# Folding two weight matrices beside the experts: operands of the first step swapped, a turn added, the first two batches' queries as a pair

## The chip, the core and the metric

The kernel runs on one core of one Trainium2 chip. The metric is the device time of one execution in microseconds (us). The core has a TensorE (PE: matmuls and turns; PEld: its weight loads), a VectorE (DVE), a ScalarE (ACT), a GpSimd (POOL) and a SyncE (SP), which here issues most DMAs.

## What is computed

Two layers on x, 8 batches of 100 tokens of 512 numbers, with a context of 361 rows of 128 numbers for each batch. Cut to what matters:

```python
x = x + L0_xattn(layernorm(x), ctx, Wq, Wkv_expand, Wout)   # 16 heads, causal, softmax
x = x + L0_ffn(layernorm(x), Wg, W1, W2, W3)                # 8 experts, each token takes its top 2
x = x + L1_xattn(layernorm(x), ctx, Wq, w_kc_q, w_kc_kv, W_qr, W_kr, Wo)
x = x + L1_ffn(layernorm(x), w_gate_up, w_down)             # rounded to 8-bit steps

# L1_xattn, the part that concerns this case, for each of 16 heads h:
q_hk  = (hidden_q @ Wq.T).reshape(b, s, H, K)               # K = 128
q_big = einsum('bshk,hkq->bshq', q_hk, w_kc_q)              # q: 384
q_r   = einsum('bshq,hqr->bhsr', q_big, W_qr)               # r: 64
```

For one head, q_r is hidden_q times Wq_h.T (512 x 128) times w_kc_q_h (128 x 384) times W_qr_h (384 x 64). None of the three weights depends on the tokens, so the kernel multiplies them first.

## The kernel before

**Tiling.** The 800 tokens stand in seven tiles of 128 rows (the last has 32). TensorE, VectorE and ScalarE run in an order written out by hand in most stages: each engine takes its instructions in the order in which the source issues them, and one that waits holds up what stands behind it on its engine. DMAs and POOL are ordered by the scheduler. `bank()` hands out one of eight PSUM banks in turn. An f32 product appears in the profile as two PE instructions, an f32 turn (a transpose, a product with `ident`) as one.

**Start.** Two products with zeros (L433) run while the first tile of x is loaded. `first_norm` normalizes tiles (statistics on DVE, square root on ACT in L238, scaling on DVE), `take_columns` turns one tile (L253) and copies it to `xnT` (ACT, L254), `keys` makes the first four batches' keys (L224, each copied by ACT in L228). `queries0(b, n)` makes the queries of n batches (L269) and copies them in two halves (ACT, L273): n = 1 moves 100 columns against each piece of `wq_sb`, n = 2 moves 200. Before, batches 0 and 1 have n = 1 each and the others n = 2. Then `first_norm(2, NT)` norms the other five tiles, and the attention of layer 0 goes batch by batch.

**Gate.** The gate's scores are made in two groups, tiles 0 to 4 and tiles 5 and 6. For each group: `gate_columns` turns the tiles (L577, copies L580 on DVE and L582 on ACT), `gate_scores` (L592, L600), `rank_choices` and `give_slots` (a chain of small DVE instructions and two products), and then two scatters for each tile (POOL, L680) put the rows into the experts' slots in DRAM. The last DVE instruction of the chain (L806) tells whether any expert has too many tokens; a branch (L886) follows, which is not taken here. Behind it the experts' rows are fetched (SP, L960).

**The fold.** Two heads are a pair, and there are eight pairs. `fold_load` brings a pair's weights (`wq_p`, `kq_p`, `qr_p`; three buffers of each). For a pair:
- first step: `fold_head` (L705), six products of w_kc_q's pieces (stationary, 128 columns) with W_qr's pieces (64 columns moving); `fold_copy` (L713) copies the result, 128 x 128, to `a_p` on ACT;
- `fold_second` (L723): two products, each into one half of the partitions, stationary `a_p` (64 columns a head), moving `wq_p` (512 columns), copied to `f_p` (ACT, L727);
- `fold_third` (L733): four turns, copied to `wqf` (ACT, L734), which the second attention's queries use.

Pair 0 is folded between the gate's two groups. Pair 1 has its first step before the branch and the rest behind it, beside pair 2. Pairs 3 to 7 are folded one in each of the experts 0 to 4:

```python
gate_and_up(0)
if loaded: part = fold_first(*loaded.pop(0)); ...
quantise_next()
gate_and_up(1)
if part: part = fold_second(*part)
...
gate_and_up(2)
quantise_next(); ... load_expert(e + 2) ...
if part: fold_third(*part)
turned = columns_of(e + 1, slots[e + 1])
```

Here `gate_and_up` makes one of three parts of an expert's hidden values (L1053, 240 columns moving; in part 2, four of its products go into halves of the partitions), `columns_of` turns the next expert's rows (L985, copies L987 on DVE and L989 on ACT), and the down products (L1117) follow. DVE rounds layer 1's weights beside it (`quantise_next`).

Of the kernel before, what the change touches and what calls it, by code (L numbers as in the profile page):

```python
# [12 lines left out]
F32 = mybir.dt.float32  # L13
# [6 lines left out]
P = 128  # L20
# [19 lines left out]
NH1, R1, CQ = 16, 64, 384  # L40
# [10 lines left out]
def tile_kernel(  # L51
# [7 lines left out]
    nc = tc.nc  # L59
# [11 lines left out]
    def bank(dtype=F32):  # L71
        cols = 512 if dtype == F32 else 1024
        return psum.tile([P, cols], dtype, tag="bank", name="bank")
# [11 lines left out]
    ident = keep.tile([P, P], F32, tag="ident", name="ident")  # L85
# [171 lines left out]
    def queries0(b, n, parts=(0, 1)):  # L257
        per = 4 // n
        if parts[0] == 0:
            qT = atw.tile([P, KC, n * S], F32, tag=f"qT{n}", name=f"qT{b}")  # L260
            for i in range(n):
                queries_of[b + i] = qT[:, :, ts(i, S)]
                halves_of[b + i] = qT
        qT = halves_of[b]
        for o0 in [per * i for i in parts if per * i < KC]:
            pq = bank()
            for o in range(o0, o0 + per):
                for c in range(KC):
                    nc.tensor.matmul(  # L269
                        pq[:, ds((o - o0) * n * S, n * S)], wq_sb[:, c, ts(o, P)],  # L270
                        xnT[:, c, ds(b * S, n * S)], start=(c == 0), stop=(c == KC - 1),
                    )
            nc.scalar.activation(  # L273
                qT[:, ds(o0, per), :], pq[:, : KC * S].rearrange("p (c q) -> p c q", c=per),
                AF.Copy, scale=1.0 / math.sqrt(HD0),
            )
# [152 lines left out]
        attn0_values(b, vals.pop(b), pT)  # L429


    for _ in range(2):
        nc.tensor.matmul(bank()[:, :384], zeros[:, :P], zeros[:, :384], start=True, stop=True)  # L433
    first_norm(0, 1)
    take_columns(0)
# [1 line left out]
    first_norm(1, 2)  # L437
    keys(0, 2, KC)
    take_columns(1)
    queries0(0, 1)  # L440
    queries0(1, 1)
    first_norm(2, NT)

    begin(0)
# [254 lines left out]
            nc.sync.dma_start(qr_p[:, j], wqr[2 * i + j].rearrange("(c p) r -> p c r", p=P))  # L699
        return i, wq_p, kq_p, qr_p  # L700

    def fold_head(i, wq_p, kq_p, qr_p, j, pa=None):
        pa = bank() if pa is None else pa
        for c in range(CQ // P):
            nc.tensor.matmul(  # L705
                pa[:, ts(j, R1)], kq_p[:, j, c, :], qr_p[:, j, c, :],
                start=(c == 0), stop=(c == CQ // P - 1),
            )
        return pa

    def fold_copy(i, wq_p, kq_p, qr_p, pa):
        a_p = fw.tile([P, 2 * R1], F32, tag="a_p", name=f"a_p{i}", bufs=2)
        nc.scalar.copy(a_p, pa[:, : 2 * R1])  # L713
        return i, wq_p, a_p

    def fold_first(*loads):
        pa = fold_head(*loads, 0)
        return fold_copy(*loads, fold_head(*loads, 1, pa))

    def fold_second(i, wq_p, a_p):  # L720
        pb = bank()
        for j in range(2):
            nc.tensor.matmul(  # L723
                pb[ds(R1 * j, R1), :], a_p[:, ts(j, R1)], wq_p[:, j, :], start=True, stop=True
            )
        f_p = fw.tile([P, D], F32, tag="f_p", name=f"f_p{i}", bufs=2)
        nc.scalar.copy(f_p, pb)  # L727
        return i, f_p

    def fold_third(i, f_p):  # L730
        pt = bank()
        for c in range(KC):
            nc.tensor.transpose(pt[:, ts(c, P)], f_p[:, ts(c, P)], ident)  # L733
        nc.scalar.copy(wqf[:, :, ts(i, P)], pt.rearrange("p (c r) -> p c r", c=KC))  # L734
# [49 lines left out]
    nc.scalar.activation(sd0[:, 0:1], ln_eps, AF.Exp)  # L784
    for t in range(5, 7):
        gate_norm(t)
    part = fold_second(*part)
    loaded.append(fold_load(pairs_left.pop(0)))
    xT = gate_columns(5, 7)
    fold_third(*part)  # L790
    gate_scores(5, 7, xT)

    loads = loaded.pop(0)
    pa = fold_head(*loads, 0)
    rank_choices(5, 7)
    give_slots(5, 7)

# [64 lines left out]
    def quantise_next():  # L862
        if gate_up_in:
            turn_gate_up(*quantise_gate_up(*gate_up_in.pop(0)))
            if gate_up_left:
                gate_up_in.append(load_gate_up(gate_up_left.pop(0)))
# [98 lines left out]
    def choices(e, got):  # L965
        gates = []
        for i, (xg, _) in enumerate(got):
            n = SLOTS[i][1]
            one = ffw.tile([P, 1], F32, tag="one", name=f"one{e}_{i}", bufs=4)[:n]
            nc.vector.tensor_scalar(one, xg[:, D + 2 : D + 3], float(NE - e), None, ALU.is_equal)  # L970
            gate = ffw.tile([P, 1], F32, tag="gate", name=f"gate{e}_{i}", bufs=4)[:n]
            nc.vector.scalar_tensor_tensor(
                gate, xg[:, D : D + 1], one, xg[:, D + 1 : D + 2], ALU.mult, ALU.add
            )
            place = small.tile([P, 1], I32, tag="place", name=f"place{e}_{i}")[:n]
            nc.vector.tensor_copy(place, xg[:, D + 3 :])
            gates.append((gate, place))
        return gates
# [55 lines left out]
    )  # L1034
    in_order.__enter__()

    part = fold_copy(*loads, fold_head(*loads, 1, pa))
    following = fold_first(*loaded.pop(0))
    part = fold_second(*part)
    following = fold_second(*following)  # L1040
    fold_third(*part)
    fold_third(*following)
    turned = columns_of(0, slots[0])
# [2 lines left out]
    for e in range(NE):  # L1046
# [10 lines left out]
        def gate_and_up(m):  # L1057
            m0, mr = HCH[m]
            pw = bank()
            s = ffw.tile([P, CAP], F32, tag="silu", name="silu")  # L1060
            if m < 2:
                products(pw[:, :CAP], ds(m0, P))
                products(pw[:, ds(CAP, CAP)], ds(UP[m], P))
                nc.scalar.activation(s, pw[:, :CAP], AF.Silu)  # L1064
                nc.vector.tensor_tensor(hT[:, m, :], s, pw[:, ds(CAP, CAP)], ALU.mult)  # L1065
                return
            products(pw[:, :CAP], ds(m0, P))
            for half in range(2):
                products(
                    pw[ds(64 * half, 64), ds(CAP, CAP)], ds(UP64, 64), 2 * half, 2 * half + 2  # L1070
                )
            nc.scalar.activation(s[:mr], pw[:mr, :CAP], AF.Silu)
            nc.vector.tensor_tensor(hT[64:mr, m, :], s[64:mr], pw[mr:, :CAP], ALU.mult)
            up = ffw.tile([64, CAP], F32, tag="up", name="up", bufs=1)
            nc.vector.tensor_copy(up, pw[:64, ds(CAP, CAP)])
            nc.vector.tensor_tensor(up, up, pw[64:, ds(CAP, CAP)], ALU.add)
            nc.vector.tensor_tensor(hT[:64, m, :], s[:64], up, ALU.mult)  # L1077
# [4 lines left out]
        part = None  # L1082
# [5 lines left out]
        quantise_next()  # L1088
        gate_and_up(1)
        if part:  # L1090
            part = fold_second(*part)
        if e < KC:
            turn_down(*quantise_down(*down_in))
            if e + 1 < KC:
                down_in = load_down(e + 1)
        gate_and_up(2)
        quantise_next()
        if e + 2 < NE:
            experts[e + 2] = load_expert(e + 2)
        else:  # L1100
            load_wo(*((0, 1, 2) if e + 2 == NE else (3, 4)))
        if part:
            fold_third(*part)
        if e == KC + 1:
            load_wo(5, 6, 7)
        if e + 1 < NE:
            turned = columns_of(e + 1, slots[e + 1])
            gates_next = choices(e + 1, slots[e + 1])

        py = [bank() for _ in range(HC)]  # L1110
        down = [(m, i) for m in range(len(HCH)) for i in range(HC)]
# [613 lines left out]
```

## Time and profile before

| what | value |
|---|---|
| time, median of 4 runs | 694.75 us (692.34 to 699.4) |
| the profiled execution: its time, its span | 694.62 us, 692.9 us |
| PE busy | 652.0 us (94% of the span) |
| DVE, ACT, POOL busy | 419.6, 245.6, 184.3 us |
| granted clock, mean over the span | 0.973 |
| start of the gate's first scatter, of the last | 117.66, 134.46 |
| start of the first expert's products | 146.71 |

Times in views are counted from the span's start. A line of a timeline has the start, the length, the engine, the line of the source, the operation, out<-in by the program's names, and the number of instructions that were merged; in brackets stands the idle time of the engine before it and what ended it. Matmuls overlap: a group of merged matmuls shows as longer than the distance to the next group. "PEclk" is the clock that TensorE was granted, in tenths of full speed, over 40 slices of the span.

### The profile page before, as it was taken

To read this page: it belongs to the slowest core of one execution; us is meant where nothing else is said; L and a number is where in the kernel's file an instruction comes from. 1 tells how busy PE (TensorE), PEld (TensorE's weight loads), DVE (VectorE), ACT (ScalarE), POOL (GpSimd) and SP (SyncE) were. 2 spreads that over 40 slices of the span, in tenths; PEclk is the share of its full clock that TensorE was granted. 3 is DMA by queue.
4 is the path that set the end of the run, shared out by engine and by line. 5 is a ranking of instruction groups with operands and counts; after the bars stand their busy time and mean duration, and the time that the engine had idled before them with its cause. 6 is when DMAs were issued, how large, how long until landed. Compare 5 with 4: busy or idle time off the path is not lost.

```text
span 692.9 us, 10202 instructions
## 1 busy us (share of the span) xinstructions
PE 652.0 (94%) x3630; PEld 421.3 (61%) x3637; DVE 419.6 (61%) x1059; ACT 245.6 (35%) x557; POOL 184.3 (27%) x197
## 2 busy tenths in 40 slices
PE   8999997499999999997899999999999999999995
PEld 6767755367766677476676666666666644444442
DVE  4775688326666452442346867876666356566687
ACT  3554454132222111330135555555555412222140
POOL 2132231601111111168114233333433202211021
PEclk9999999589999999999799999999999999999999
DMA  8700293699999997744010210210000030111211
GB/s 300 232 17 18 96 331 113 232 304 249 309 262 323 317 255 194 186 140 127 22 16 1 57 42 16 57 34 11 2 12 1 3 125 8 29 28 29 48 34 63
DMA packets 80312, 80.41 MB, mean 116 GB/s; under 512 B 41283, under 2 KB 54135, under 8 KB 80127
## 3 DMA queue, kind: packets, MB, share of 16 engines
q1 hardware_dynamic: 76543, 70.97, 35.3%
q0 software_dynamic: 3712, 8.72, 5.7%
q8 instruction: 30, 0.49, 0.3%
q14 instruction: 27, 0.22, 0.1%
HBM read 56.36 MB, written 16.50 MB: 105 GB/s over the span
## 4 chain that ended last, share of the span: by engine, by line
PE 65%; DVE 7%; DMA 2%; POOL 2%; issue 2%; ACT 1%; SPq 1%; ACTq 0%; POOLq 0%; DVEq 0%
PE bank L357 11%; PE bank L1053 11%; PE bank L1330 10%; PE bank L1310 7%; PE bank L1267 6%; PE bank L1117 6%; PE bank L1324 4%; PE bank L1453 3%; POOL e L1318 2%; PE bank L1300 2%; PE bank L705 1%; DVE nm L1312 1%; PE bank L723 1%; PE bank L985 1%; DMA x_acc<-y,place 1%
## 5 line engine op out<-in xcount | busy, mean ns | idle before, releaser
L1318 POOL TENSOR_SCALAR e<-e,rs 128x361 f32<-128x361 f32 (+1 forms) x56 | 66.9, 1196 | 146.3 <-DVE rs L1317 146.3
L357 PE MATMUL bank<-wvo,ctxT 128*128 128x512 f32 x192 | 83.9, 593 | 0.0
L1310 PE MATMUL bank<-kvT,qe 128*128 128x361 f32 (+1 forms) x208 | 82.0, 477 | 0.0
L1053 PE MATMUL bank<-xgT,w 128*128 128x240 f32 (+1 forms) x384 | 76.4, 370 | 0.9 <-ACT xgT L989 0.9
L1053 PEld LDWEIGHTS bank<-xgT,w 128*128 128x128 f32 (+1 forms) x384 | 63.9, 181 | 15.5 <-issue 9.9
L1330 PE MATMUL bank<-pT,kvr 121*128 121x400 f32 x192 | 70.4, 502 | 1.8 <-DVE pT L80 1.8
L1315 ACT ACTIVATE e<-bank,nm 128x361 f32<-128x361 f32 (+1 forms) x104 | 58.8, 565 | 29.3 <-DVE nm L1312 20.5
L1312 DVE TENSOR_REDUCE nm<-bank 128x1 f32<-128x361 f32 (+1 forms) x104 | 54.9, 528 | 21.6 <-PE bank L1310 20.4
L1324 PEld LDWEIGHTS bank<-ident,e 128*121 128x121 f32 (+1 forms) x312 | 47.3, 183 | 33.8 <-POOL e L1318 7.3
L357 PEld LDWEIGHTS bank<-wvo,ctxT 128*128 128x128 f32 x192 | 36.2, 190 | 43.1 <-issue 42.6
L1128 POOL DMA_INDIRECT x_acc<-y,place x16 | 24.4, 1526 | 126.1 <-ACT y L1127 122.9
L1324 PE MATMUL bank<-ident,e 128*121 128x128 f32 (+1 forms) x312 | 52.7, 279 | 2.1 <-POOL e L1318 2.1
L1470 POOL TENSOR_TENSOR hid<-g,u 128x512 f32<-128x512 f32 (+1 forms) x17 | 20.5, 1213 | 111.1 <-ACT g L1461 74.8
L1330 PEld LDWEIGHTS bank<-pT,kvr 121*128 121x128 f32 x192 | 33.9, 190 | 21.4 <-issue 1.9
L1267 PE MATMUL bank<-xT,wqf 128*128 128x256 f32 (+1 forms) x192 | 45.5, 399 | 0.7 <-ACT xT L1252 0.7
L322 POOL TENSOR_TENSOR s<-s,rs 100x800 f32<-100x800 f32 x16 | 24.4, 1523 | 72.6 <-DVE rs L321 30.5
L1117 PE MATMUL bank<-w,hT 128*128 128x512 f32 (+3 forms) x96 | 43.0, 595 | 0.3 <-DVE hT L1077 0.3
L1267 PEld LDWEIGHTS bank<-xT,wqf 128*128 128x128 f32 x192 | 37.4, 196 | 7.9 <-ACT xT L1252 0.9
L1310 PEld LDWEIGHTS bank<-kvT,qe 128*128 128x128 f32 (+1 forms) x208 | 32.5, 186 | 9.4
L82 ACT COPY pT<-bank 121x384 f32<-121x384 f32 (+1 forms) x51 | 23.8, 466 | 32.1 <-PE bank L1324 31.5
L80 DVE COPY ctxT<-bank 128x400 f32<-128x400 f32 (+2 forms) x23 | 13.1, 573 | 33.1 <-PE bank L1267 23.8
L1065 DVE TENSOR_TENSOR hT<-silu,bank 128x240 f32<-128x240 f32 x16 | 6.5, 404 | 39.5 <-ACT silu L1064 39.5
(251 smaller groups left out, 1036.6 us busy)
## 6 DMA issues: line engine op xcount, KB each, us to landing
w<-in_w SPq DMA_DIRECT2D x8, 1408.0 KB
gu<-in_wgu SPq DMA_DIRECT2D x22, 256.0 KB
w<-in_w SPq DMA_DIRECT2D x16, 256.0 KB
wq_p<-in_wq SPq DMA_DIRECT2D x8, 512.0 KB
wo<-in_wo SPq DMA_DIRECT2D x8, 512.0 KB
x_slot<-zeros SPq DMA_DIRECT2D x1, 3840.0 KB
kq_p<-in_wkcq SPq DMA_DIRECT2D x16, 192.0 KB
dn<-in_wdn SPq DMA_DIRECT2D x4, 704.0 KB
```

The source lines that it names most:

```text
L322: nc.gpsimd.tensor_tensor(part, part, rs.unsqueeze(2).to_broadcast([S, 8, S]), ALU.mult)
L357: nc.tensor.matmul(po[:, :D], lhs[:, c, ds(t * P, r)], rhs[:, c, :], start=(c == 0), stop=(c == chunks - 1),)
L1053: nc.tensor.matmul(po, w12_e[:, c, cols], xgT[:, c, :], start=(c == c0), stop=(c == c1 - 1))
L1117: nc.tensor.matmul(py[i][:n], hT[:mr, m, ds(s0, n)], w3_e[:mr, m, :], start=(m == 0), stop=(m == 2))
L1128: d = nc.gpsimd.indirect_dma_start(out=x_acc, out_offset=bass.IndirectOffsetOnAxis(ap=place[:, 0:1], axis=0), in_=y, in_offset=None, compu ...
L1267: nc.tensor.matmul(pq[:, i, :], wqf[:, c, ts(p0 + i, P)], xT[:, c, :], start=(c == 0), stop=(c == KC - 1),)
L1310: nc.tensor.matmul(ps[:r, :L], qe[:, ds(k0, r)], kvT, start=True, stop=True)
L1312: nc.vector.tensor_reduce(nm[:r], ps[:r, :L], AX.X, ALU.max, negate=True)
L1315: nc.scalar.activation(e[:r], ps[:r, :L], AF.Exp, bias=nm[:r], accum_out=sm[:r])
L1318: (nc.vector if odd else nc.gpsimd).tensor_scalar_mul(e[:r], e[:r], rs[:r])
L1324: nc.tensor.transpose(pt[:LP, c, :r], e[:r, ds(c * (LP - 1), LP)], ident[:r, :r])
L1330: nc.tensor.matmul(pc[:, :VC], kvr[:, c, :], pT[:, c, ts(j, VC)], start=(c == 0), stop=(c == LC - 1))
```

## The change

- Three products with zeros at the start instead of two.
- `queries0(0, 2)` instead of `queries0(0, 1)` and `queries0(1, 1)`.
- The fold's first step has its operands swapped: W_qr's pieces are stationary (64 columns) and w_kc_q's move (128 columns), and the two heads' products go into the two halves of the partitions. The result comes out turned; it is copied to `t_p`, turned by TensorE in a new step, `fold_turn`, and copied to `a_p`. All later steps are the same.
- Places: pair 0's turn stands just ahead of its `fold_second`, whose own place is kept, between `gate_norm` and `gate_columns` of tiles 5 and 6. Pair 1 has its whole first step before the branch, its turn behind it. In the experts the turn takes `fold_second`'s place behind `gate_and_up(1)`, `fold_second` comes behind `gate_and_up(2)`, and `fold_third` behind `columns_of` and `choices`.

```diff
-    for _ in range(2):
+    for _ in range(3):
         nc.tensor.matmul(bank()[:, :384], zeros[:, :P], zeros[:, :384], start=True, stop=True)
 ...
     take_columns(1)
-    queries0(0, 1)
-    queries0(1, 1)
+    queries0(0, 2)
     first_norm(2, NT)
 ...
+    def fold_first(i, wq_p, kq_p, qr_p):
+        pa = bank()
         for c in range(CQ // P):
-            nc.tensor.matmul(
-                pa[:, ts(j, R1)], kq_p[:, j, c, :], qr_p[:, j, c, :],
-                start=(c == 0), stop=(c == CQ // P - 1),
-            )
+            for j in range(2):
+                nc.tensor.matmul(
+                    pa[ds(R1 * j, R1), :P], qr_p[:, j, c, :], kq_p[:, j, c, :],
+                    start=(c == 0), stop=(c == CQ // P - 1),
+                )
+        t_p = fw.tile([P, P], F32, tag="t_p", name=f"t_p{i}", bufs=1)
+        nc.scalar.copy(t_p, pa[:, :P])
+        return i, wq_p, t_p
+
+    def fold_turn(i, wq_p, t_p):
+        pa = bank()
+        nc.tensor.transpose(pa[:, :P], t_p, ident)
+        a_p = fw.tile([P, P], F32, tag="a_p", name=f"a_p{i}", bufs=2)
+        nc.scalar.copy(a_p, pa[:, :P])
         return i, wq_p, a_p
 ...
     for t in range(5, 7):
         gate_norm(t)
-    part = fold_second(*part)
+    part = fold_second(*fold_turn(*part))
     loaded.append(fold_load(pairs_left.pop(0)))
     xT = gate_columns(5, 7)
 ...
-    loads = loaded.pop(0)
-    pa = fold_head(*loads, 0)
+    part = fold_first(*loaded.pop(0))
     rank_choices(5, 7)
 ...
-    part = fold_copy(*loads, fold_head(*loads, 1, pa))
+    part = fold_turn(*part)
     following = fold_first(*loaded.pop(0))
     part = fold_second(*part)
-    following = fold_second(*following)
+    following = fold_second(*fold_turn(*following))
 ...
         gate_and_up(1)
         if part:
-            part = fold_second(*part)
+            part = fold_turn(*part)
 ...
         gate_and_up(2)
+        if part:
+            part = fold_second(*part)
         quantise_next()
 ...
-        if part:
-            fold_third(*part)
         if e == KC + 1:
             load_wo(5, 6, 7)
         if e + 1 < NE:
             turned = columns_of(e + 1, slots[e + 1])
             gates_next = choices(e + 1, slots[e + 1])
+        if part:
+            fold_third(*part)
```

## The prediction

> **What bounds the kernel now.** I read the page first, then the timelines of the four places that the change touches: the start, the end of the gate, the stretch behind the branch, and one expert. All times are us from the span's start; line numbers are those of the kernel before.
>
> ```profile
> PE 652.0 (94%) x3630; PEld 421.3 (61%) x3637; DVE 419.6 (61%) x1059; ACT 245.6 (35%) x557; POOL 184.3 (27%) x197
> PEclk9999999589999999999799999999999999999999
> ```
>
> TensorE is busy for 94% of the span, so most of its time is on the path. The clock row dips at the eighth slice (about 121 to 138): there TensorE had been idle and the clock was halved. Tables of stretches give a granted clock of 0.50 from 119.8 to 143.6 and 1.00 from 143.7.
>
> The timeline of the first expert:
>
> ```profile
> 150.03 1.45 PE L705 MATMUL bank<-qr_p,kq_p 128*128 128x64 f32 x12
> ...
> 151.31 3.46 PE L1053 MATMUL bank<-xgT,w 128*128 128x240 f32 x16
> ...
> 154.70 1.08 PE L723 MATMUL bank<-wq_p,a_p 128*64 128x512 f32 x4
> ...
> 155.71 2.85 PE L1053 MATMUL bank<-xgT,w 128*128 128x240 f32 x16
> ...
> 158.50 0.66 PE L733 MATMUL bank<-ident,f_p 128*128 128x128 f32 x4
> ...
> 164.98 3.40 PE L1053 MATMUL bank<-xgT,w 128*128 128x240 f32 x16
> ...
> 168.22 1.45 PE L705 MATMUL bank<-qr_p,kq_p 128*128 128x64 f32 x12
> ```
>
> Each starts when the one before has streamed: no row waits for another engine. An expert lasts 18.2 (150.03 to 168.22), and what the fold costs here is on the path. (An f32 product is two instructions, so six products are x12.)
>
> The end of the gate, all engines:
>
> ```profile
> 117.14 0.27 ACT L713 COPY a_p<-bank 128x128 f32<-128x128 f32 x1 [2.41 <-PE bank L705]
> ...
> 119.98 1.28 ACT L784 ACT_TABLE_LOAD   x1
> ...
> 120.80 1.68 PE L577 MATMUL bank<-ident,x_all 128*128 128x128 f32 x8 [2.26 <-DVE x_all L559]
> ...
> 121.38 0.57 ACT L727 COPY f_p<-bank 128x512 f32<-128x512 f32 x1
> ...
> 130.76 0.96 POOL L680 DMA_INDIRECT x_slot<-x_all,to  x1 [0.33 <-DVE tmp L670]
> ```
>
> L577 turns tiles 5 and 6 for the gate; from it a chain over scores, ranks and slots leads to the eleventh scatter at 130.76. The scatters ahead of it stand 0.30 apart and this one 0.33, ended by DVE: the chain has no slack. The branch (L886) and the fetch of rows at 137.5 stand behind it.
>
> Behind the branch, and the start:
>
> ```profile
> 137.12 2.79 PE L705 MATMUL bank<-qr_p,kq_p 128*128 128x64 f32 x12 [8.20 <-issue]
> ...
> 139.84 3.74 PE L723 MATMUL bank<-wq_p,a_p 128*64 128x512 f32 x8
> 139.99 1.28 ACT L713 ACT_TABLE_LOAD   x1 [11.41 <-PE bank L705]
> ...
> 143.51 1.47 PE L733 MATMUL bank<-ident,f_p 128*128 128x128 f32 x8
> ```
>
> ```profile
> 6.64 4.79 PE L224 MATMUL bank<-ctx,wkv_sb 128*128 128x400 f32 x8
> ...
> 11.70 7.29 PE L269 MATMUL bank<-xnT,wq_sb 128*128 128x100 f32 x64
> ...
> 11.90 0.59 ACT L254 COPY xnT<-bank 128x512 f32<-128x512 f32 x1
> ...
> 19.42 0.29 ACT L238 ACTIVATE sd<-mv,ln_eps 128x5 f32<-128x5 f32 x1
> ...
> 23.52 2.92 PE L224 MATMUL bank<-ctx,wkv_sb 128*128 128x400 f32 x8 [0.20 <-PE bank L253]
> 27.98 5.68 PE L269 MATMUL bank<-xnT,wq_sb 128*128 128x200 f32 x32
> ```
>
> The eight products of L224 take 4.79 at the start and 2.92 later: TensorE starts at half speed, until 10.6 by their spacing. VectorE's norms (and then its score work, nearly without a gap) wait for L238 at 19.42, which stands in ScalarE's queue behind the last copy of L273.
>
> **Start: pair of queries and third product.** The pair removes 64 steps of 0.11 (11.70 to 18.82: 7.1) and adds 32 steps of 0.17 (27.98 to L331 at 33.49: 5.4). But it needs both tiles' columns, so it starts behind the copy at 11.90, at 12.55, and ends at 18.0: gain 0.8, not 1.7, and L238 follows. The third product is two instructions of 0.64 (1.51 to 4.07 holds four). It ends at 5.35, before L253 at 5.76 (which waits for DVE), so it costs nothing; if x came over 0.4 earlier it would cost the rest. What it may bring is the clock. The clock rose twice in rows I can weigh. The stretch 136.8 to 140.2 streams 49% of its time (12 x 0.107 of L705 plus 0.4 of L723) and brought nothing; 140.2 to 143.6 streams 93% and was followed by full speed. At the start 3.7 to 7.1 streams 54% now, and brought nothing; with the third product 88%. That is nearest to the 93%, so I take full speed at 7.1: some five steps of L224 at 0.33 instead of 0.67 bring its second kT copy, L238 of tile 1, its transposes and copy forward; the pair starts at 11.3 and ends at 16.7, gain 2.0. Bounds -0.8 and -2.05; taken **-2.0**.
> A rule of the Trainium skill speaks against this: in "TensorE: Matmul & The Clock Gate", section "PE-mode transpose", transposes do not count as busy for the gate; then 62% of the stretch counts, and the sum below would be 1.2 higher by it. No row here shows transposes alone.
>
> **Gate: a second trip through ACT.** fold_first is copied once more (t_p), turned, and copied again (a_p). By the program's order this a_p copy stands in ScalarE's queue behind L784, so behind two table loads: it runs when f_p did, 121.38 to 121.65 instead of 117.14. fold_second waits for it on TensorE at 121.70, and L577 is queued behind fold_second. At half speed fold_second takes 1.76 (139.84 to 141.60), so L577 starts at 123.55 instead of 120.80: **+2.7**; at full speed (1.01) +1.9. What is late next: gT copies, scores, ranks, scatters 11 to 14, the branch, the fetch of rows. SP's load of wq_p moves behind fold_second, hidden (used at 154.7).
>
> **Behind the branch.** The turn of pair 1 is first; a_p needs ScalarE's table load (1.28) and copy: fold_second starts at 139.25, 0.6 earlier than now, because fold_first in halves (1.3 at half speed instead of 2.7) lies beside the table load. But pair 2's a_p copy stands behind pair 1's f_p copy (141.2 to 141.8): its fold_second starts at 142.1 instead of 141.60. From there it is the clock: full speed from 140.2 gives -0.8 at L985, from 143.6 +0.3, only from 147 +1.6. The first stretch would stream 73%, midway between 54 and 93; taken **+0.4**. The rows of expert 0 are no cover: they land by 141.1, while L985 starts at 144.81.
>
> **Experts 0 to 4.** A step of 240 columns is 0.2025 (164.98 to 168.22: 16 steps). L1053 and L723 together take 4.40 (151.31 to 155.71); less 16 steps, 1.16 for L723. L1117's steps of 512 columns are 0.43, so four in a row would be 1.72: its column halves run in pairs (2 x 0.43 = 0.86), and 0.30 is entering and leaving the halves. In gate_and_up(2) the same (155.71 to 158.50, less 12 steps: 0.36).
> - fold_first: 6 pairs of 128 columns, 0.11 each (0.2025 x 128/240), 0.65, plus 0.33 for in and out, 0.98 against 1.28: -0.30. Weight loads of 64 columns are shorter than the step.
> - one turn: +0.11 (L733's step); its t_p copy has all of gate_and_up(1), 3.2, as cover.
> - fold_second behind gate_and_up(2), already in halves: -0.30.
> - fold_third behind columns_of: same work; the f_p copy (0.59) lies beside columns_of (0.9), nothing; without cover 0.7.
> Sum -0.49, five times: **-2.45**. If halves ran one after another: 1.65 for fold_first, +0.9 in all; if entering were free, -4.1. The DMA queues are near full here (share 1.0 to 1.1), but the fourth expert's weights, the tightest, land at 215.0 for use at 219.6, so 2.5 is hidden.
> The skill's "TensorEngine Tiling (Array Packing)", section "When to Use Tiling", gives up to twice the speed for this swap; by it fold_first would be 0.64 and the sum 1.7 lower. Its "Key Properties" say that a change of mode drains the array, and the 0.30 is the size of that here.
>
> **Sum.** -2.0 + 2.7 + 0.4 - 2.45 = -1.35 on the profiled 694.62 (span 692.9 and 1.7 around it, 0.1 under the median of 694.75): **693.3**. With the bounds: -2.05 + 1.9 - 0.8 - 4.1 = -5.05 (689.6) and -0.8 + 2.75 + 1.6 + 0.9 = +4.45 (699.1).
>
> **Rivals.**
> - *Slower: ScalarE's queue decides.* Place: a_p behind L784 and the clock that stays low behind the branch. -0.8 + 2.75 + 1.6 - 2.45 = +1.1, 695.7. For it: no slack at 130.76, and the third product's 88% is a guess. Against: 73% may be enough. It decides once gate and branch cost more than the 3.3 of pair and experts.
> - *The late gate is hidden.* Landings of the scatters trail their issues by 3 to 7, and TensorE's branch ends at 136.85 beside them; if the queue of scatters, not the chain, ends last, the 2.7 goes: 690.6. Against: the branch's flag (L806) is at the end of the same chain.
> - *The halves don't overlap* (the change doesn't do what it says): +0.9 instead of -2.45, 696.6. Against: L723's 1.16.
>
> **How the numbers follow.** Forecast 0.50, slower rival 0.28, hidden gate 0.14, no overlap 0.08. The forecast's own range is 691.5 to 695.0; both signs together, and runs that spread from 692.3 to 699.4, give 689.0 to 699.5. A measurement of this kernel tells about 1% from no change, 6.9 us; no case reaches it by its sum alone, so faster by more than that gets 0.07, slower 0.10 (a clock that stays low into expert 0), within it 0.83.
>
> **What would show it.** Right: L224 in about 3.5; L269 x32 from 11.3; L577 some 2.7 later against the first scatter; L1053, fold_first, L1053 with 1.0 between; an expert of 17.7. Wrong: an expert of over 18.2, L577 not behind fold_second, or the eleventh scatter still 0.33 behind the tenth.

## The result, and the profile after

The median of after is 693.7 us (52 runs) against 694.57 (78 runs): a ratio of 0.9989, 95% interval 0.9977 to 1.0002. That is no difference. The prediction said 693.3. The ratio leaves out eight of the upper times, which count as slow (over 1.5% above the fastest of after, 688.08); with them the mean of after is 694.65, that of before 694.55.

The median hides something. The 78 times of before form one group. Of the 52 of after, 30 lie from 688.1 to 694.8 and 22 from 696.0 to 700.2, with none between. The profiled execution (695.52 us, span 693.8) lies between the two, so it stands for neither; read it beside the execution of before (694.62, span 692.9).

| stretch (us, in the two profiled executions) | before | after | difference |
|---|---|---|---|
| span's start to the gate's first scatter | 117.66 | 116.24 | -1.42 |
| first scatter to the branch's flag (`spilt`) | 13.61 | 16.19 | +2.58 |
| flag to TensorE's first product behind the branch | 5.85 | 5.79 | -0.06 |
| that product to expert 0 | 9.59 | 8.35 | -1.24 |
| experts 0 to 4 | 91.04 | 93.63 | +2.59 |
| expert 5 to the second attention's first queries | 61.04 | 61.04 | 0 |
| these to its first scores | 59.17 | 57.51 | -1.66 |
| scores to the end | 334.92 | 335.00 | +0.08 |

They add up to +0.87, the difference of the spans. The page of after, first the busy times, then the granted clock in 40 slices:

```profile
PE 646.4 (93%) x3608; PEld 413.9 (60%) x3615; DVE 419.2 (60%) x1059; ACT 247.5 (36%) x565; POOL 184.1 (27%) x197
PEclk9999998599999999999799999999999999999999
```

TensorE is busy 5.6 less than before (652.0), yet the span is not shorter: it waits more. Now the timelines of after, place by place (start, length, engine, line, out<-in, count; in brackets the idle time and what ended it). The start:

```profile
1.51 3.72 PE L433 MATMUL bank<-zeros 128*128 128x384 f32 x6 [1.51 <-POOL zeros L161]
5.71 0.63 PE L253 MATMUL bank<-ident,xn 128*128 128x128 f32 x4 [0.49 <-DVE xn L244]
7.39 2.92 PE L224 MATMUL bank<-ctx,wkv_sb 128*128 128x400 f32 x8 [1.05 <-DMA ctx<-in_ctx_t]
7.95 0.69 DVE L234 BATCH_NORM_STATS2 stats<-x 128x6 f32<-128x512 f32 x1 [2.38 <-DMA x<-in_x]
11.92 5.68 PE L269 MATMUL bank<-xnT,wq_sb 128*128 128x200 f32 x32 [0.67 <-ACT xnT L254]
18.04 0.29 ACT L238 ACTIVATE sd<-mv,ln_eps 128x5 f32<-128x5 f32 x1
```

L224 now takes 2.92 instead of 4.79: the clock is already full. But here the context and the second tile of x landed late (L224 waits 1.05 for the one, L234 starts at 7.95 instead of 6.91 for the other), and L269 starts at 11.92. L238, the norms' gate, is 1.4 earlier than before (19.42).

The end of the gate:

```profile
115.24 0.27 ACT L710 COPY t_p<-bank 128x128 f32<-128x128 f32 x1 [1.93 <-PE bank L705]
115.53 1.28 ACT L238 ACT_TABLE_LOAD   x1
118.56 1.28 ACT L784 ACT_TABLE_LOAD   x1
119.96 0.25 ACT L717 COPY a_p<-bank 128x128 f32<-128x128 f32 x1
120.26 1.97 PE L723 MATMUL bank<-wq_p,a_p 128*64 128x512 f32 x4 [4.37 <-ACT a_p L717]
122.16 1.68 PE L576 MATMUL bank<-ident,x_all 128*128 128x128 f32 x8
131.92 0.95 POOL L679 DMA_INDIRECT x_slot<-x_all,to  x1 [2.91 <-DVE tmp L669]
```

The copy to `a_p` stands behind both table loads, L723 waits 4.37 for it, and the turns of the last two tiles (L576) stand behind L723. They start 5.92 behind the first scatter (116.24); in before it was 3.14. The eleventh scatter now waits 2.91 for the chain instead of 0.33.

Behind the branch:

```profile
135.98 1.28 ACT L717 ACT_TABLE_LOAD   x1 [6.33 <-issue]
138.22 0.45 PE L715 MATMUL bank<-ident,t_p 128*128 128x128 f32 x1 [7.93 <-issue]
138.70 0.27 ACT L717 COPY a_p<-bank 128x128 f32<-128x128 f32 x1 [1.44 <-PE bank L715]
139.93 1.62 PE L723 MATMUL bank<-wq_p,a_p 128*64 128x512 f32 x4
142.41 1.08 PE L723 MATMUL bank<-wq_p,a_p 128*64 128x512 f32 x4 [0.60 <-ACT a_p L717]
```

The table load that before had waited for a product (139.99) now runs ahead of TensorE's restart, and the second L723 takes 1.08, at full speed: the clock's own record has it full from 141.1, 2.9 behind the restart, where before it took 6.5.

One expert without a stall (expert 1):

```profile
164.25 3.40 PE L1052 MATMUL bank<-xgT,w 128*128 128x240 f32 x16
167.59 0.88 PE L705 MATMUL bank<-kq_p,qr_p 128*64 128x128 f32 x12
168.39 3.51 PE L1052 MATMUL bank<-xgT,w 128*128 128x240 f32 x16
171.74 0.27 PE L715 MATMUL bank<-ident,t_p 128*128 128x128 f32 x1
171.84 2.75 PE L1052 MATMUL bank<-xgT,w 128*128 128x240 f32 x16
174.42 1.03 PE L723 MATMUL bank<-wq_p,a_p 128*64 128x512 f32 x4
175.39 1.04 PE L984 MATMUL bank<-ident,xg 128*128 128x128 f32 x8
176.27 0.60 PE L733 MATMUL bank<-ident,f_p 128*128 128x128 f32 x4
176.71 5.32 PE L1118 MATMUL bank<-w,hT 128*128 128x512 f32 x12
181.86 0.37 PE L1052 MATMUL bank<-xgT,w 128*128 128x240 f32 x1
```

17.61 from start to start, against 18.19. But expert 3, from 200.12, takes 22.03:

```profile
212.65 3.60 PE L1118 MATMUL bank<-w,hT 128*128 128x512 f32 x8
213.38 1.62 DVE L145 TENSOR_REDUCE amax<-dn 128x1 f32<-128x1408 f32 x1 [4.64 <-DMA dn<-in_wdn]
218.63 0.40 DVE L1076 TENSOR_TENSOR hT<-silu,up 64x240 f32<-64x240 f32 x1
219.08 3.27 PE L1118 MATMUL bank<-w,hT 96*128 96x512 f32 x4 [2.83 <-DVE hT L1076]
```

VectorE waits 4.64 for `dn`, a piece of layer 1's weights that it only rounds here. In its written order the last part of `hT` (L1076) stands behind that, and TensorE's last down products need it. In before the same reduction had no wait:

```profile
210.16 1.61 DVE L145 TENSOR_REDUCE amax<-dn 128x1 f32<-128x1408 f32 x1
```

SyncE's own queue shows where the 4.64 began. (`w2q` is the rounded `dn`, turned by a DMA.) Before, then after:

```profile
199.84 1.49 SPq L150 DMA_TRANSPOSE w2q<-dn_q  x1
201.38 0.79 SPq L828 DMA_DIRECT2D dn<-in_wdn  x1
...
204.20 0.38 SPq L483 DMA_DIRECT2D w<-in_w  x1
```

```profile
201.88 0.40 SPq L482 DMA_DIRECT2D w<-in_w  x1
202.37 5.02 SPq L150 DMA_TRANSPOSE w2q<-dn_q  x1
207.45 0.59 SPq L827 DMA_DIRECT2D dn<-in_wdn  x1
```

The scheduler, which orders SyncE's instructions, now puts the large load of the next expert's `w12` in front of the turn of `w2q` and the load of `dn`. The load of `w12` itself holds SyncE for only 0.40, but the turn of `w2q` behind it takes 5.02 instead of 1.49. In the four profiles that have `w12` in front, the second and third turns of `w2q` take 3.0 to 5.0; in the ten others 1.4 to 1.7, but for one of 3.6. So `dn` is issued 7.3 behind the start of its expert instead of at its start. The tables of stretches for experts 1 to 3 (window, length, busy times, clock, share of the DMA engines, GB/s) add that in expert 2, while this delay built up, the queues were full and slow, 249 GB/s:

```profile
164.25:181.86 17.61, 17.61 (x91) 12.36 (x89) 11.83 (x29) 3.98 (x10) 3.15 (x2) 1.00 1.10 302
181.86:200.12 18.26, 17.77 (x90) 12.19 (x89) 11.30 (x25) 4.00 (x10) 3.39 (x3) 1.00 1.21 249
200.12:222.15 22.03, 19.19 (x90) 12.70 (x90) 12.20 (x33) 3.97 (x9) 3.19 (x3) 0.94 1.13 331
```

### The profile page after: what moved, and what is told of

Its sections match the earlier page's. It is cut to its first block, busy times and chain, and to the rows that moved or that the text cites. A ratio compares the mean times of both kernels' runs of the same rounds, so it can differ in the third digit from the quotient of the medians.

```text
span 693.8 us, 10174 instructions
## 1 busy us (share of the span) xinstructions
PE 646.4 (93%) x3608; PEld 413.9 (60%) x3615; DVE 419.2 (60%) x1059; ACT 247.5 (36%) x565; POOL 184.1 (27%) x197
## 4 chain that ended last, share of the span: by engine, by line
PE 63%; DVE 8%; DMA 3%; issue 2%; POOL 2%; ACT 1%; SPq 1%; ACTq 0%; POOLq 0%; DVEq 0%
PE bank L357 11%; PE bank L1052 10%; PE bank L1331 10%; PE bank L1311 7%; PE bank L1268 6%; PE bank L1118 5%; PE bank L1325 4%; PE bank L1454 3%; POOL e L1319 2%; PE bank L1301 2%; DVE nm L1313 1%; PE bank L984 1%; PE bank L723 1%; DMA dn<-in_wdn 1%; DMA cos_sb<-in_rope_cos 1%
## 5 line engine op out<-in xcount | busy, mean ns | idle before, releaser
L1052 PE MATMUL bank<-xgT,w 128*128 128x240 f32 (+1 forms) x384 | 76.4, 371 | 1.4 <-ACT xgT L988 0.9
L1052 PEld LDWEIGHTS bank<-xgT,w 128*128 128x128 f32 (+1 forms) x384 | 64.3, 182 | 14.1 <-issue 5.8
L1118 PE MATMUL bank<-w,hT 128*128 128x512 f32 (+3 forms) x96 | 44.5, 611 | 3.1 <-DVE hT L1076 3.1
L1118 PEld LDWEIGHTS bank<-w,hT 128*128 128x128 f32 (+3 forms) x96 | 17.0, 186 | 24.2 <-issue 16.9
```

The lines of the kernel that those rows point to most:

```text
L1052: nc.tensor.matmul(po, w12_e[:, c, cols], xgT[:, c, :], start=(c == c0), stop=(c == c1 - 1))
L1118: nc.tensor.matmul(py[i][:n], hT[:mr, m, ds(s0, n)], w3_e[:mr, m, :], start=(m == 0), stop=(m == 2))
```

## The experiments

Each is compared with runs of before beside it; those had medians of 698.5 to 698.8, so only ratios are compared across. The theories: *order*, `dn` is late because of where SyncE issues it; *full queues*, a shorter expert outruns the transfers whatever the order; for the gate, *a_p behind the table loads*.

### Is it the order of the loads?

`sp_as_before`: after, with SyncE's order in experts 0 to 4 tied to that of before.

```diff
-            experts[e + 2] = load_expert(e + 2)
+            if e in (1, 2):
+                with tc.issue_after(gu_load[0]):      # the last load of gu
+                    experts[e + 2] = load_expert(e + 2)
+            else:
+                experts[e + 2] = load_expert(e + 2)
```

(`fold_load` and `load_wo(5, 6, 7)` are tied to the last `w3` load in the same way, as they moved up otherwise.)

> The kernel after, with the loads of layer-0 expert weights, fold weights and output weights tied behind other loads so that SyncE issues everything in experts 0 to 4 in the order of the kernel before (the w12 load of the next-but-one expert behind the turn of w2q, the load of dn and the second gu, not ahead of them). TensorE, VectorE and ScalarE keep the order of after. Theory A (order of issue): dn came late in after (VectorE waited 5.7 for it in two places, 0 in before) only because w12 was put ahead of it, so now VectorE waits 0 for dn, each of experts 0 to 4 lasts 17.6 to 17.7 (after: 17.68, 17.61, 18.26, 22.03, 18.05; before: 18.2 each), experts 0 to 4 together 88.4 instead of 93.6, and the time falls by about 5 against after, to some 688.5; the stretch of norms at 324 to 331 may give back or take up to 1.5. Rival B (the DMA queues are full, and a shorter expert only outruns them): in the new order another tile comes late instead, the five experts last 91 or more together, and the time stays at 692 to 694.

Ratio 0.9939 (0.9914 to 0.9964). Experts 0 to 4: 17.68, 17.61, 17.61, 17.61, 17.64, together 88.15. One wait for `dn` is left, 0.7, which costs 0.03. The twelve times are one group, 692.7 to 698.3. The experts came as expected, the whole did not: beside the 0.9977 of after (`after_again`, below) 0.9939 is 2.7 less, not 5, since not every execution of after has the long wait.

`w12_ahead_in_before`: the other way about, before with the `w12` loads of experts 3 and 4 in front.

```diff
 ...
         gate_and_up(2)
+        if e in (1, 2):
+            early, w12_load = load_w12(e + 2)
+            with tc.issue_after(w12_load):
+                turn_down(*down_q)
+                down_in = load_down(e + 1)
 ...
```

> The kernel before, with one change: in experts 1 and 2 SyncE issues the w12 load of the next-but-one expert ahead of the turn of w2q, the load of dn and the second turn of w1q, as in after. Nothing else moves on any engine. Theory A (order of issue): dn is now issued some 7 behind the start of an expert instead of at its start and lands some 13 into it, while VectorE wants it at 8.8; VectorE waits 3 to 5 for dn in one or two experts, hT and the down products come late, those experts last 1 to 4 longer than 18.2, and the time rises by 2 to 5 against before, to 697 to 699. Rival B (only a shorter expert outruns the full queues): experts of 18.2 leave the queues their time, no wait on dn over 1, time as before (694.6 within 1).

A miss in the profile: no wait, experts of 18.2. But this execution hardly tests the theory, because `dn` was not issued late in it. Expert 3 starts at 204.86 here, and SyncE issues the fourth `dn` 0.31 behind that, not 7:

```profile
201.62 0.38 SPq L483 DMA_DIRECT2D w<-in_w  x1
...
205.17 0.63 SPq L833 DMA_DIRECT2D dn<-in_wdn  x1
```

It landed at 213.57 for use at 213.66, 0.09 in hand, where before had 3.4. The ratio is 1.0032 (0.9999 to 1.0066), and the times fall apart: eight from 697.4 to 700.6 and four from 703.1 to 707.6, where only two of 35 runs of before beside it are above 702. The ratio's interval reaches 1, so this is a hint and not a proof: the order takes the slack away, and whether a wait follows differs between executions. The four upper times were not profiled.

`after_again`: after itself once more.

> The kernel after, unchanged, beside the others of this call. In the profile of after VectorE waited 5.7 for dn and experts 0 to 4 took 93.6; with the same order of SyncE's loads the kernel early_turn waited 0 and took 88.1. So the wait is not in every execution. Theory A (the order of issue leaves no slack for dn, and whether it is late depends on how fast the transfers run in that execution): the times fall in two groups some 4 to 6 apart, as the 52 known times of after do (30 at 688.1 to 694.8, 22 at 696.0 to 700.2, none between), with a third to a half in the upper one; the profiled execution shows either 88.1 and no wait, or a wait of 3 to 6 on dn. Rival B (that one profile was an accident): one group, and 88.1.

Ratio 0.9977 (0.9947 to 1.0007). Two groups again: five times from 692.5 to 694.9, seven from 697.0 to 702.9. In the profile `dn` is waited for once, 2.9, and expert 3 lasts 19.85. This execution, with 694.87, belongs to the lower group. So a wait of this size doesn't yet put an execution into the upper group, and no execution of the upper group was profiled.

`dn_ahead`: after with a second buffer for `dn`, each piece loaded one expert earlier.

```diff
-        w = qin.tile([P, NI], F32, tag="dn", name=f"dn{n}", bufs=1)
+        w = qin.tile([P, NI], F32, tag="dn", name=f"dn{n}", bufs=2)
 ...
-    down_in = load_down(0)
+    down_in = [load_down(0), load_down(1)]
 ...
```

> The kernel after with two buffers for dn instead of one, the second loaded before the experts and each later one an expert earlier than before. SyncE's order then has the w12 loads behind dn as well, by itself. Theory A (dn late is the whole of the loss in the experts): VectorE never waits for dn, experts 0 to 4 take 88.1 to 88.5, one group of times, ratio as that of the order alone (0.994 of before). Rival B (another transfer comes late in the place of dn, since the queues are full): another wait of 1 or more in experts 0 to 4, or two groups of times again.

Ratio 0.9939 (0.9920 to 0.9959), all six times between 693.5 and 695.4, experts 0 to 4 in 88.11. The view of the tile `dn` has nothing under its waits:

```profile
L145 DVE TENSOR_REDUCE amax<-dn x4: 1610/1612/1614, 157.7 to 210.5; 128x1 f32<-128x1408 f32 x4
...
its engine sat idle before it (us, times) until:
```

With the second buffer the scheduler also puts `w12` behind `dn` again, so the two edits are not independent; what they share is that `w12` does not stand in front of `dn`. Both give 0.9939, beside 0.9977 of after in the same set as `dn_ahead`; these intervals touch, but the upper times are gone. Of the 50 times of the five kernels with `w12` behind `dn` (`sp_as_before`, `dn_ahead` and the three built on them) none is above 698.4; of the 24 of `after_again` and `early_turn`, where it stands in front, seven are. (The medians of before beside all of these are 698.5 to 698.8.) Where the fourth `dn` landed, counted from the start of its expert, by the last of its transfers:

| profiles | landed behind the expert's start | wanted at |
|---|---|---|
| fold and order of before: before, `start_alone`, `third_alone`, `pair_alone` | 4.9 to 5.8 | 8.8 |
| the same: `before_again` | 9.9 | 8.8 |
| fold of before, `w12` in front: `w12_ahead_in_before` | 8.7 | 8.8 |
| fold of after, order of before: `sp_as_before`, `order_and_turn` | 9.2, 10.1 | 8.5 |
| fold of after, `w12` in front: after, `after_again`, `early_turn` | 13.2, 11.4, 7.5 | 8.5 |

*Order* holds: the long waits are where `w12` stands in front. *Full queues* holds too, in a smaller way: with the order of before there are waits of 1.0 (`before_again`), 0.7 and 1.6, and the last made an expert of 18.47. The fourth `dn` stands at its margin in either order, and how fast it lands differs between executions.

### The gate, and what hides it

`early_turn`: after with pair 0's turn in front of the table loads.

```diff
-    part = fold_first(*loaded.pop(0))
+    part = fold_turn(*fold_first(*loaded.pop(0)))
     project_add(5, po)
 ...
-    part = fold_second(*fold_turn(*part))
+    part = fold_second(*part)
```

> The kernel after, with pair 0's turn (L715) and its copy to a_p placed directly behind its first step, so ahead of the Sqrt and Exp table loads in ScalarE's queue; fold_second keeps its place. Theory (the gate pays for a_p standing behind two table loads): the a_p copy runs at about 116 instead of 119.96, fold_second no longer waits, the turns of tiles 5 and 6 (L576) start some 3.1 behind the first scatter as in before instead of 5.92, the eleventh scatter stands about 0.3 behind the tenth instead of 2.91, and the branch's flag (spilt) is some 2.5 earlier, near 129.8. At the end of the run 1 to 2.5 earlier than after (691 to 692.5), since the clock behind the branch and the late dn of experts 2 and 3 may move. Rival (the chain to the branch is bound elsewhere, by scatters or by VectorE): the eleventh scatter and the flag move by under 0.5, the time stays at 693.7.

The first half is as expected, the second is not:

```profile
115.19 0.27 ACT L717 COPY a_p<-bank 128x128 f32<-128x128 f32 x1 [0.42 <-PE bank L715]
115.48 1.28 ACT L238 ACT_TABLE_LOAD   x1
115.50 1.23 POOL L679 DMA_INDIRECT x_slot<-x_all,to  x1 [15.89 <-DVE tmp L669]
118.73 1.06 PE L576 MATMUL bank<-ident,x_all 128*128 128x128 f32 x8 [2.14 <-DVE x_all L558]
...
122.80 1.55 PE L705 MATMUL bank<-kq_p,qr_p 128*64 128x128 f32 x12
...
128.44 0.27 ACT L710 COPY t_p<-bank 128x128 f32<-128x128 f32 x1 [6.42 <-remote]
...
131.30 0.96 POOL L679 DMA_INDIRECT x_slot<-x_all,to  x1 [3.04 <-DVE tmp L669]
```

L576 starts 3.23 behind the first scatter: the price of the table loads is gone. Then something new decides. L705, pair 1's first step, ends by its records at 124.35, but ScalarE's copy of it, which waits for TensorE alone, starts at 128.44; "remote" says that no record explains the release. ScalarE's next instruction is the gate's, so the chain waits, the scatter is 3.04 late again, and the flag is 16.31 behind the first scatter, as in after (16.19). The ratio is 0.9952 (0.9921 to 0.9982).

`before_again`: is that lag the kernel's?

> The kernel before, unchanged, one look. The four profiles of the last call have TensorE's results 1.8 to 4 later than its own records in front of the branch, the profiles of before and after not, and the median of before beside that call was 698.5 instead of 694.6. If that lag belongs to where a kernel is run and not to the kernel, this profile either shows it (ScalarE's a_p copy of pair 1 some 3 to 4 behind the end of L705, span near 696) or the call's median of before is near 694.6 and it does not.

It is there in before as well: L705's copy waits 6.5, ended by "remote", and the flag is 16.4 behind the first scatter instead of 13.6. So the lag is not of the changed kernel, and before has it in the later runs. In this profile the flag is 2.8 later and the whole 1.9 longer (696.54 against 694.62), less than the 4 by which their medians are higher; the rest is open. The profiles with the lag come from all three chips of the experiments (7, 11 and 3).

`order_and_turn`: the order of `sp_as_before` and the turn of `early_turn` together.

> After with both edits: SyncE's order of loads in experts 0 to 4 as in before, and pair 0's turn directly behind its first step. Theory A with the gate's price: no wait on dn and one group of times; the gate's 2.8 is gone too where nothing else ends last in front of the branch, so 2 to 3 below the order alone (0.9939 of before), near 0.990 of before. Rival: what stands in front of the branch (in three of the last four profiles TensorE's results came 1.8 to 4 later than its records say) takes the 2.8, and the kernel equals the order alone, 0.994 of before. In the profile: L576's turns some 3.2 behind the first scatter, experts of 17.6, no wait on dn.

Ratio 0.9936 (0.9915 to 0.9957), the rival's answer: as the order alone. L576 is 3.23 behind the first scatter and the flag 17.50; in `sp_as_before` 5.94 and 17.77. Of the gate's 2.7 only 0.3 reaches the flag between these two, and 0.2 between `dn_ahead` (17.71) and `dn_ahead_and_turn` (17.54). It is not always so: between `after_again` (18.60) and `early_turn` (16.31) it is 2.3.

`dn_ahead_and_turn`: the two edits of `dn_ahead` and `early_turn`.

> After with two buffers for dn (as in dn_ahead) and pair 0's turn directly behind its first step (as in early_turn). Theory: no wait on dn, experts 0 to 4 of 17.6, one group of times; L576 some 3.2 behind the first scatter. Where TensorE's results come late in front of the branch, as in seven of the ten profiles so far, that lag hides the gate's 2.8, and the kernel equals dn_ahead, 0.994 of before; where they do not, 0.990. Rival (the early turn has a price of its own, for instance in the clock behind the branch, which stayed halved until 146.8 in early_turn): above dn_ahead by 1 or more, 0.996.

Ratio 0.9935 (0.9915 to 0.9955): the same again. One expert lasts 18.52: `dn_q`, which has one buffer, waited 1.7 for a late turn of `w2q`.

`pair1_behind`: that kernel with pair 1's first step behind the branch.

```diff
-    part = fold_first(*loaded.pop(0))
+    later = loaded.pop(0)
     rank_choices(5, 7)
 ...
-    part = fold_turn(*part)
+    part = fold_turn(*fold_first(*later))
```

> The kernel dn_ahead_and_turn with pair 1's first step (six pairs of products and the copy to t_p) moved from in front of the branch to behind it, just ahead of its turn. Question: is the lag of TensorE's results in front of the branch (products of pair 1 end by their records at 124.4 and the semaphore is only raised at 128.4, in early_turn) a matter of these products, or of that stretch? If of the products (their weights or their bank): the lag is gone, spilt comes 2 to 4 earlier, the branch too, 0.7 of first step is paid behind it, and the time is 1.5 to 3 below dn_ahead_and_turn. If of the stretch: ScalarE or VectorE waits for the next results instead (parts, nb or most), spilt stays within 0.7, and the time rises by 0.5 to 1.5.

The lag is gone and the flag comes at 129.81 instead of 133.01. But the time is the same, 0.9942 (0.9920 to 0.9963), and that part of the expectation was wrong: from TensorE's restart to expert 0 it takes 13.78 instead of 8.68. The added first step has a table load behind it (137.49), TensorE waits, and the clock is full only at 148.0 instead of 143.3. So in this one profile the lag is gone with these products; before and after have them there too and show no lag. Why TensorE's signal comes late stays open. The record shows one pattern: in ten of the eleven profiles with the lag the signal comes 12.9 to 14.7 behind the first scatter, so 0.2 to 1.9 behind the end of the tenth, whether the products end 8.9 or 12.7 behind the first scatter (in `start_alone` it comes at 11.4). Earlier products do not bring an earlier signal there.

### The start

`start_alone`: before with three products with zeros and the pair.

> The kernel before with only the start of after: three products with zeros, and the queries of batches 0 and 1 as a pair. In the profile of after the first scatter came 1.4 earlier than in before (116.24 against 117.66), where the prediction had 2.0. Theory: the start is worth 1.4 at the first scatter and nothing behind it depends on when it comes, so the time is 1.4 below before, near 693.2. Rival: the gain is lost in the clock's windows behind the branch or in the wait for norms at 324 to 330 of before (5.96), and the time is as before within 0.5. The clock rises to full at 4.6, L269 starts at 11.9.

Ratio 0.9964 (0.9940 to 0.9988). Clock full from 4.5, L269 at 11.0, first scatter 2.3 earlier than in before; the gain reaches the time (2.5 less, 0.8 to 4.2 by the interval, where 1.4 was expected).

`third_alone` and `pair_alone`: the two halves of it.

> The kernel before with three products with zeros instead of two and nothing else. The prediction's start of 2.0 was 0.8 for the pair and 1.2 for a clock that rises earlier. Three profiles without the third product have the clock full from 9.0 to 10.5 and the first maximum of scores (L308) at 21.9 to 22.3; seven with both edits from 4.5 to 7.4 and 19.6 to 20.9. If the two parts add: clock full by 7.4, first maximum at 20.9 (1.2 earlier). Rival (the rise comes with the pair's place, not with the product): clock at 9 to 10.5, first maximum at 22.1.

> The kernel before with the queries of batches 0 and 1 as a pair and nothing else. If the two parts add: clock full from 9.0 to 10.5 as before, first maximum of scores at 21.3 (0.8 earlier). Rival (the pair waits for the second tile as long as it saves): first maximum at 22.1.

The first maximum of scores (L308) stands at 21.9 to 22.3 in three profiles of kernels with the old start, and at 19.6 to 20.9 in nine with the new one, on average 22.10 and 20.11: -2.0. The third product alone: clock full from 5.1, first maximum at 20.94, -1.2 as expected. The pair alone: clock at 10.75, first maximum at 21.77, -0.3 instead of -0.8 (its second tile of x was at VectorE 0.5 later than in before, 7.43 against 6.91).

## Why the prediction was right, and where it was not

The total was right, and in good part by luck: misses of opposite signs cancel in part. Against its terms the profiled execution lost 5.0 in the experts and 0.6 at the start, and gained 1.6 behind the branch. It also gained 1.7 behind the experts, where the prediction had no term. Between the means of all times there is no gain at all.

- **Start, -2.0.** Right: -2.0 over twelve profiles; the -1.4 of after's own is late landings of x and ctx. The clock rose because of the third product, as worked out (`third_alone`), at 4.5 to 7.4 where 7.1 was taken. The pair's 0.8 is not confirmed: alone it brought 0.3, in one profile.
- **Gate, +2.7.** Right in mechanism and size: L576 came +2.78 later against the first scatter in after, and `early_turn` took it away. The rival "the late gate is hidden" was worth more than its 0.14, in another form: late signals from TensorE cover most of it in several of the later runs. Whether the scatters are behind these signals is not shown. Between the two profiles without the lag, before and after, it is carried: +2.58 at the flag.
- **Behind the branch, +0.4 (-0.8 to +1.6).** Measured -1.24 in after, -0.9 to -1.2 in four others, and +0.5 and +0.9 in `dn_ahead` and `early_turn`. Two terms were mis-sized. The table load was set on the path (1.28); ScalarE did it while TensorE was idle, and the first `fold_second` starts 1.71 behind the restart instead of 2.13. The larger part is the clock, rightly named as what decides: it was full 2.9 behind the restart, and the prediction's own figure for a rise that early was -0.8. The prediction took a stretch of 73%, "midway". Up to the end of the run, the stretches of the clock record last whole multiples of 3.41 (in before 119.76 to 143.65, 23.89, is seven of them), so the share of a window of 3.41 that TensorE streams can be counted from its columns. 74% (`early_turn`, `pair1_behind`) brought no rise, 79% (after, `order_and_turn`) did, and 75% did not in `dn_ahead` and did in `dn_ahead_and_turn`. So the limit lies near 75%, and this count is not fine enough to say where. The same work falls on either side by where the window begins.
- **Do turns count for the clock?** The prediction left that open, with 1.2 at stake. In `after_again` the window from 119.84 to 123.25 was followed by full speed, at 123.25, though it holds only these two groups and the start of another turn:

```profile
119.69 1.98 PE L723 MATMUL bank<-wq_p,a_p 128*64 128x512 f32 x4 [4.36 <-ACT sd L784]
121.60 1.68 PE L576 MATMUL bank<-ident,x_all 128*128 128x128 f32 x8
```

  The products (L723) stream 46% of it and the turns 33%; `dn_ahead` has the same, 45% and 34%. Without the turns 46% would have to be enough, but 49% of products alone (before, 136.8 to 140.2) and 66% (`start_alone`, 137.6 to 141.0) brought nothing. So turns count here.
- **Experts, -0.49 each.** Right: -0.58 in every one without a stall. By its parts in expert 1: up to the second L1052 the first step saves 0.38 (predicted 0.30); turn and moved second step together save 0.19 (predicted 0.30 less 0.11); columns and third step cost nothing. The halves do overlap.
- **"so 2.5 is hidden".** This sentence failed. It took the expert's own weights as the tightest transfer (4.6 in hand). By the last of its transfers `w12` had 3.8 (215.76 for 219.56), and `dn` was tighter: in before its fourth piece landed at 206.7 for use at 210.2, 3.4 in hand, and it has one buffer and a place in VectorE's order ahead of `hT`. And it took SyncE's order as given, though moving the fold's steps changed when the scheduler issues `w12` (the kernels with only the new start keep the old order; which of the fold's steps did it was not tried alone). The cost: 2.6 instead of -2.45 in the profiled execution, where expert 3 alone lost 4.4 against its 17.6. That the upper 22 of the 52 times are such waits is inferred: they are gone where `w12` stands behind `dn`.
- **The slower rival** (ScalarE's queue and the clock decide) named the gate's half rightly and the clock's wrongly.
- **Nothing behind the experts.** After's profiled execution gave back 1.66 between 299 and 358, which no step had. There TensorE waits for a norm (L116) that stands on VectorE behind a late load of `gu`, for which VectorE waits 13.99 in before and 13.64 in after; the scaling itself took 1.76 and 0.62. Before and then after:

```profile
330.06 1.09 PE L1251 MATMUL bank<-ident,xn 128*128 128x128 f32 x4 [5.96 <-DVE xn L116]
```

```profile
330.70 1.09 PE L1252 MATMUL bank<-ident,xn 128*128 128x128 f32 x4 [4.14 <-DVE xn L116]
```

That stretch lasts 56.9 to 61.1 over all profiles and does not order the kernels, so it is scatter, not a gain.

So the change gains where `dn` is in time, and loses much of that where it is not. The lower 30 times of after have a median of 692.5, 2.1 below before (all of it, not its lower part); in the later runs, where the lag often hides the gate's cost, the kernels with `w12` behind `dn` are 0.6% below, 4.3. The version to keep is `dn_ahead`: 0.9939 of before (0.9920 to 0.9959), beside 0.9977 of after (0.9947 to 1.0007).

## What to carry to other kernels

Where an order is half written by hand and half planned, moving a compute step also moves loads that it does not touch: compare the issue order of every queue, and list the slack of each transfer in the stretch that gets shorter, the single-buffered ones and those that only side work needs first of all. The order alone does not tell what a transfer costs, either: the turn behind the large load held SyncE for 5.02 instead of 1.49. A step that needs one more trip through an engine pays for whatever already stands in that engine's queue, here two table loads. And when a profile is one execution, look at the spread of the times before explaining it: two groups of times can mean a wait that is sometimes there, and one profile can miss it.

## What was not expected of the hardware

- TensorE's signals came up to 5.6 late, against the modelled ends of its products, in one stretch just ahead of the branch (all profiles of the experiments but that of `pair1_behind`; not those of before and after), with products recorded as done at their usual pace. With pair 1's products moved out of it the lag was gone, in one profile. The cause is open.
- The clock's rise behind the branch: windows of 3.41 that streamed 74% did not bring it, windows of 79% did, and of two with 75% one did (worked out from the columns in the records). From TensorE's restart to expert 0 it took 8.35 to 8.68 with the early rise, 10.08 and 10.51 with one a window later. Turns counted like products.
- An activation table load can run ahead of the wait of the instruction that it stands before: at 135.98, 2.2 ahead of TensorE's restart.
